# Cross-attention and a mixture of experts on one core: the last group's four pairs of sends, each begun half a tile after the one before

## The chip, the core and the metric

The kernel runs on one core of a Trainium2 chip. The metric is the time of one execution on the device in microseconds; lower is better. The core's engines are called PE (matrix multiply; PEld is its loading of weights), DVE (vector), ACT (scalar), POOL (GpSimd) and SP (which here only issues DMAs). Each runs its own list of instructions in order, and they wait for each other through semaphores.

## The reference

Eight sequences of 256 rows of 256 numbers pass through a gated cross-attention and then a gated mixture of experts. Everything is float32.

```python
# _L0_ffn_ref: x is (8, 256, 256), W1 (8, 1024, 256), W2 (8, 256, 1024), Wr (8, 256)
logits = jnp.einsum('btd,ed->bte', x, Wr)
probs = jax.nn.softmax(logits / TEMPERATURE, axis=-1)
topk_vals, topk_idx = jax.lax.top_k(probs, TOPK)            # TOPK = 2 of 8 experts
router_weights = topk_vals / topk_vals.sum(-1, keepdims=True)
one_hot = jax.nn.one_hot(topk_idx, E, dtype=x.dtype)
gate = jnp.einsum('btk,btke->bte', router_weights, one_hot)
h = jax.nn.silu(jnp.einsum('btd,efd->btef', x, W1))
y = jnp.einsum('btef,edf->bted', h, W2)
out = jnp.einsum('bte,bted->btd', gate, y)

# the whole
x = x + jnp.tanh(g_xattn[0]) * _L0_xattn_ref(_layernorm(x), ctx_1024, ...)
x = x + jnp.tanh(g_ffn[0]) * _L0_ffn_ref(_layernorm(x), W1, W2, Wr)
```

The attention (16 heads, 120 context rows) comes first and is not touched by the change. In the second half the reference runs all experts for all 2048 tokens and weighs them; only two of eight weights of a token are not zero.

## The kernel before

**Routing.** The kernel computes an expert only for the tokens that chose it. Tokens are handled in four groups of 512 (`g` from 0 to 3; the last is `g = NG - 1 = 3`). For a group, `logits` and `router` choose two experts for each token. `places` (L302 to L380) then works out the row that each token gets in the list of each of its two experts, and sends the token's normalised row (256 numbers, its gates and its number) to that row of the table `routed` in DRAM. A list has 2048 rows for each expert.

A send is an indirect DMA on POOL (L366) that scatters 128 rows. There are eight for a group: two halves `h` of the group, for each the first and the second choice, for each two blocks of 128 tokens. `places` is a generator. Each step of it makes one reduction on DVE (L362, row numbers of two blocks, tile `slot0` or `slot1`), issues the two sends that use it, and yields. So a group is four steps of one reduction and two sends; below, the four pairs are S1, S2, S3 and S4. The code ahead of the first reduction (counts by two matmuls, gates, row numbers) runs in the first step.

**Tiles of the second half.** The loop at L1213 goes over `order`, tiles of 128 rows of one expert. The first eight are the first 128 rows of each expert's list (`"first"`); the lists are laid out so that these rows are filled by the groups 0 and 1, and their loads are declared independent of later sends. From `i = 8` on come `"full"` tiles, whose place in the lists and whose expert are known only when all groups are counted: `table()` (L710) works them out on DVE in four steps, the first up to L737, the second from L670 to L744 with the tiles `full_row` and `expert_i`, and two more for the rest of the rows. Their loads (`load`, L845 and L852 on SP) read `full_row` into a register and must come after all sends.

One pass `i` of the loop, in the order of the code:

- L1241 `go_up()`: up projection of tile `i`, 16 matmuls (L897), and its Silu on ACT (L905)
- L1255 `open_tile(i + 1)`: the rows of the next tile are transposed on DVE (L884); for a full tile its expert's weights are copied first (L864)
- L1259: for `i` 5 and 8, a step of the table
- L1274 `close_tile()`: down projection of tile `i - 1`, 8 matmuls (L913), scaling by the gate on DVE (L921), and the sum into the output by an indirect DMA on POOL (L938, `add_up`)
- L1284: for `i` 3 and 4, two steps of the last group's sends
- L1287: for `i` 4, the first step of the table
- L1296: loads of tiles up to four ahead, on SP

The order of the instructions of PE, DVE, ACT and SP is that of the code. POOL has no order of its own written out; it too ends up with its instructions in the order in which the code makes them. So before the change POOL has, from pass 3 on: sum of tile 2, S1, S2, sum of tile 3, S3, S4, sum of tile 4, sum of tile 5. Each sum waits for the landing of the sum before it. DVE has the reductions of S1 and S2 directly one behind the other after the gates (pass 3), and those of S3 and S4 behind the scaling of tile 3 and ahead of the table's first step (pass 4).

Of the kernel before, what the change touches and what calls it, by code (L numbers as in the profile page):

```python
# [49 lines left out]
def tile_gated_xattn_moe(  # L50
# [356 lines left out]
    def load_expert(e):  # L407
        nc.sync.dma_start(
            part(e, 0, DC, DFF), w1T[e].rearrange("(c p) f -> p c f", p=P)
        )  # L410
        nc.sync.dma_start(
            part(e, DC * DFF, FC, D), w2T[e].rearrange("(c p) d -> p c d", p=P)
        )
# [231 lines left out]
    def turn_y(b, bank):  # L645
        g, i = b // 2, b % 2
        rows, xn2T = groups[g]
        turned(xn2T[:, :, ts(i, N)], [rows[i][:, k, :D] for k in range(2)], f"f{b}", bank)
# [161 lines left out]
    def load(t):  # L810
        kind, i = t
        xt = take(fp, [P, XW], "xt", f"xt_{kind}{i}", bufs=6)
        if kind == "first":
            for first in load_blocks(xt, i * T):
                for send in behind:
                    tc.declare_no_dep(
                        first.ins, send.ins, reason="rows behind those of the first tiles"
                    )
                firsts.append(first)
            return xt  # L820
        if kind == "quad":
            nc.gpsimd.indirect_dma_start(
                out=xt,
                out_offset=None,
                in_=routed[:, :],
                in_offset=bass.IndirectOffsetOnAxis(
                    ap=tables[1][0][:, i : i + 1], axis=0
                ),
            )
            return xt  # L830
        start = nc.sync.value_load(
            tables[0][1][0:1, i : i + 1], min_val=0, max_val=NOWHERE
        )
        load_blocks(xt, start)
        return xt
# [19 lines left out]
    def weights(t, xt):  # L855

        kind, i = t
        if kind != "full":
            w2 = part(i, DC * DFF, FC, D)
            return part(i, 0, DC, DFF), xt[:, D + i : D + i + 1], lambda: w2  # L860
        expert_i = tables[0][0]
        e = nc.vector.value_load(expert_i[0:1, i : i + 1], min_val=0, max_val=E - 1)
        w1 = take(fw[0], [P, DC, DFF], "w1", f"w1_{i}")
        nc.vector.tensor_copy(  # L864
            w1.rearrange("p c f -> p (c f)"),
            w_sb[:, ds(e, 1), : DC * DFF].rearrange("p e f -> p (e f)"),
        )
        gate = take(fw[3], [P, 1], "gate", f"gate_{i}", bufs=4)
        nc.vector.tensor_copy(gate, xt[:, D : D + E][:, ds(e, 1)])

        def copy_w2():
            w2 = take(fw[0], [P, FC, D], "w2", f"w2_{i}")
            nc.vector.tensor_copy(
                w2.rearrange("p c d -> p (c d)"),
                w_sb[:, ds(e, 1), DC * DFF :].rearrange("p e f -> p (e f)"),
            )
            return w2

        return w1, gate, copy_w2

    def turn(t, xt):
        if t[0] != "quad":
            xT = take(fp, [P, DC, P], "xT", f"xT_{t[0]}{t[1]}")
            nc.vector.transpose(xT.rearrange("p c n -> p (c n)"), xt[:, :D])  # L884
            return xT
        tr = take(ps_tr, [P, DC, P], "tr", f"xtT_{t[0]}{t[1]}")
        for c in range(DC):
            nc.tensor.transpose(tr[:, c, :], xt[:, ts(c, P)], ident)
        xT = take(fp, [P, DC, P], "xT", f"xT_{t[0]}{t[1]}")
        nc.vector.tensor_copy(xT, tr)  # L890
        return xT

    def up(t, xT, w1):
        ph = take(fw[1], [P, FC, P], "ph", f"ph_{t[0]}{t[1]}")
        for f in range(FC):
            for c in range(DC):
                nc.tensor.matmul(  # L897
                    ph[:, f, :],
                    lhsT=w1[:, c, ts(f, P)],
                    rhs=xT[:, c, :],  # L900
                    start=(c == 0),
                    stop=(c == DC - 1),
                )
        hT = take(fw[3], [P, FC, P], "hT", f"hT_{t[0]}{t[1]}")
        nc.scalar.activation(hT, ph, AF.Silu)  # L905
        return hT
# [3 lines left out]
    def down(t, hT, gate, xt, w2):  # L910
        py = take(fw[2], [P, 512], "mm", f"py_{t[0]}{t[1]}")
        for f in range(FC):
            nc.tensor.matmul(  # L913
                py[:, :D],
                lhsT=hT[:, f, :],
                rhs=w2[:, f, :],
                start=(f == 0),
                stop=(f == FC - 1),
            )
        y = take(fw[3], [P, D], "y", f"y_{t[0]}{t[1]}")  # L920
        nc.vector.tensor_scalar(y, py[:, :D], gate, None, ALU.mult)  # L921
        add_up(t, y, xt)
# [125 lines left out]
    def open_tile(t, xt):  # L1048
        state["ready"] = t, xt, weights(t, xt), turn(t, xt)
# [6 lines left out]
    def go_up():  # L1056

        t, xt, (w1, gate, _), xT = state["ready"]
        return t, up(t, xT, w1), gate, xt
# [8 lines left out]
    picked, sending = {}, {}  # L1068
# [32 lines left out]
    for s, (b, o, nb) in enumerate(units):  # L1101
        k = 2 * o + nb
        n = b + 1
        g = b // 2 - 1
# [107 lines left out]
    g = NG - 1  # L1212
    for i, t in enumerate(order):  # L1213
        if i == 12:

            with tc.If(more > 0):  # L1216
                spare = {}
                for j in range(SPARE):
                    tj = ("full", j)
                    xt = load(tj)  # L1220
                    w1, gate, copy_w2 = weights(tj, xt)
                    w2 = copy_w2()
                    down(tj, up(tj, turn(tj, xt), w1), gate, xt, w2)
                for j in range(MIXED, QUADS):
                    for _ in quad(j, load(("quad", j))):
                        pass
                spare = None
        if i == 10:
            more = nc.values_load(tables[1][3][0:1, 0:1], min_val=0, max_val=FULLS)
        w2_of = state["ready"][2][2]  # L1230
        if i == 2:
            turn_y(B - 1, bank_tr)

        mixed = mix <= i < mix + 4 * MIXED
        if i == mix - 1:
            quads = [quad(j, xt) for j, xt in enumerate(quad_xts)]
        if mixed and i % 4 == 0:
            running = quads[(i - mix) // 4]
        if mixed and i > mix:
            next(running)  # L1240
        new = go_up()  # L1241
        if i == mix - 1:
            next(quads[0])
        copies = []
        if i == 1:
            for k in range(2):
                copies.append(wide_out(B - 1, k, ps_py))
        if i == 2:
            lg = logits(g, groups[g][1], bank_tr)
            next(lg)  # L1250
        for k, copy in enumerate(copies):
            copy()
            norm_y(B - 1, k)
        if i + 1 < len(order):
            open_tile(order[i + 1], xts[i + 1])  # L1255
        if mixed:
            next(running)

        if i in (5, 8):  # L1259
            tables.append(next(parts))  # L1260
        if i == 6:
            next(parts)
        if i == 0:
            norms_y.finish()
            weigh(B - 1, 1, ps_py)
            load_expert(4)
            turn_y(B - 2, bank_tr)
            sending[g - 1] = places(g - 1, groups[g - 1][0], picked[g - 1], bank_tr)
        if i == 3:
            sending[g] = places(g, groups[g][0], picked[g], bank_tr)  # L1270
        w2 = w2_of()
        if i == 1:
            norms_y.finish()
        close_tile()  # L1274
        state["pending"] = *new, w2
        if mixed:
            next(running)
        if i == 2:
            lg = next(lg)
            picked[g] = router(g, lg)  # L1280
        if i < 2:
            for _ in range(2):
                next(sending[g - 1])
        if 2 < i < 5:  # L1284
            for _ in range(2):
                next(sending[g])
        if i == 4:  # L1287
            parts = table()
            next(parts)
            routing_pool.close()  # L1290
            qp.append(
                ctx.enter_context(
                    tc.tile_pool(name="quads", bufs=1, side="right", reuse_waits="tile")
                )
            )
        while len(xts) <= min(i + AHEAD, len(order) - 1 if tables else 7):  # L1296
            xts[len(xts)] = load(order[len(xts)])
        if i == mix - 4:
            quad_xts = [load(("quad", j)) for j in range(MIXED)]
        if i == 1:  # L1300
            load_expert(3)
            load_expert(7)
# [44 lines left out]
```

## Time and profile before

| | |
|---|---|
| median of 3 runs | 538.94 us (537.75 to 539.55) |
| the profiled execution | 538.01 us |
| its span on the core | 536.30 us |
| mean granted PE clock in it | 0.992 |
| instructions | 10503 |
| sends (L366) | 32, 995 ns mean on POOL |
| sums of first and full tiles (L938) | 31, 1552 ns at the least |

A row of a timeline gives the start and the duration of a group of instructions in microseconds from the start of the span, the engine, the source line, the operation, what it writes and reads, the count, and in brackets the idle time of the engine ahead of it with what ended it. "issue" means that the profile shows nothing that the engine waited for. "SPq" is SP issuing a DMA; the transfer itself goes on after that. A POOL row of a send or a sum is the time in which POOL makes the transfer's descriptors, not the transfer.

The granted clock is the share of its full clock that PE was allowed. Of the page, two rows give it over the whole span, in 40 slices of 13.4 us:

```
PE   8999999999999999999999998999999999999992
PEclk9999999999999999999999998999999999999998
```

### The profile page before, as it was taken

To read this page: it belongs to the slowest core of one execution; us is meant where nothing else is said; L and a number is where in the kernel's file an instruction comes from. 1 tells how busy PE (TensorE), PEld (TensorE's weight loads), DVE (VectorE), ACT (ScalarE), POOL (GpSimd) and SP (SyncE) were. 2 spreads that over 40 slices of the span, in tenths; PEclk is the share of its full clock that TensorE was granted. 3 is DMA by queue.
4 is the path that set the end of the run, shared out by engine and by line. 5 is a ranking of instruction groups with operands and counts; after the bars stand their busy time and mean duration, and the time that the engine had idled before them with its cause. 6 is when DMAs were issued, how large, how long until landed. Compare 5 with 4: busy or idle time off the path is not lost. (4 is left out here: it accounts for less than half of the span.)

```text
span 536.3 us, 10503 instructions
## 1 busy us (share of the span) xinstructions
PE 520.9 (97%) x3636; PEld 438.5 (82%) x3636; DVE 283.9 (53%) x683; ACT 220.1 (41%) x700; POOL 127.8 (24%) x135
## 2 busy tenths in 40 slices
PE   8999999999999999999999998999999999999992
PEld 7788887878878788787889996999997787889991
DVE  3675656567765567744673446444544454443530
ACT  1666546464554654557630310111144554601110
POOL 2011100000332003310013445222331224234332
PEclk9999999999999999999999998999999999999998
DMA  8999990140420501012059784333322221422321
GB/s 294 333 308 309 299 261 24 46 151 2 165 93 31 188 2 40 32 41 41 2 174 376 224 240 85 44 44 45 45 41 31 32 33 16 49 36 26 44 27 20
DMA packets 82156, 57.57 MB, mean 107 GB/s; under 512 B 42864, under 2 KB 77168, under 8 KB 82096
## 3 DMA queue, kind: packets, MB, share of 16 engines
q1 hardware_dynamic: 75200, 47.36, 31.9%
q0 software_dynamic: 6480, 8.81, 9.3%
q10 hardware_dynamic: 416, 0.66, 0.4%
q8 instruction: 30, 0.49, 0.4%
q14 instruction: 30, 0.25, 0.1%
HBM read 28.67 MB, written 28.27 MB: 106 GB/s over the span
## 5 line engine op out<-in xcount | busy, mean ns | idle before, releaser
L575 ACT ACTIVATE pr<-psc,mx 128x120 f32<-128x120 f32 x256 | 88.8, 373 | 65.3 <-DVE mx L569 63.3
L897 PEld LDWEIGHTS ph_full<-xT_full,w 128*128 128x128 f32 x736 | 85.1, 192 | 6.4 <-issue 5.0
L897 PE MATMUL ph_full<-xT_full,w 128*128 128x128 f32 x736 | 86.8, 276 | 0.3 <-PEq L1216 0.3
L913 PE MATMUL py_full<-w,hT_full 128*128 128x256 f32 x368 | 83.1, 379 | 0.0
L913 PEld LDWEIGHTS py_full<-w,hT_full 128*128 128x128 f32 x368 | 68.2, 190 | 8.4
L525 PE MATMUL pq<-xnT,w_sb 128*128 128x256 f32 x256 | 62.7, 388 | 0.4 <-DVE xnT L208 0.4
L938 POOL DMA_INDIRECT out_dram<-y_full,xt_full x23 | 38.9, 1691 | 99.2 <-DVE y_full L921 65.3
L905 ACT ACTIVATE hT_full<-ph_full 128x1024 f32<-128x1024 f32 x23 | 23.5, 1023 | 94.1 <-PE ph_full L897 94.1
L619 PE MATMUL pw<-w_sb 128*128 128x256 f32 x256 | 58.5, 382 | 0.0
L575 ACT ACTIVATION_READ_ACCUMULATOR pr<-psc,mx 128x1 f32 x256 | 55.8, 218 | 0.0
L525 PEld LDWEIGHTS pq<-xnT,w_sb 128*128 128x128 f32 x256 | 46.6, 190 | 10.8 <-issue 3.1
L619 PEld LDWEIGHTS pw<-w_sb 128*128 128x128 f32 x256 | 47.7, 190 | 9.0 <-issue 2.5
L563 DVE TENSOR_REDUCE mx<-psc 128x8 f32<-128x960 f32 x32 | 37.0, 1155 | 31.3 <-PE psc L555 31.3
L366 POOL DMA_INDIRECT routed<-rows,slot x32 | 31.8, 995 | 55.7 <-DVE slot L362 49.0
L921 DVE TENSOR_SCALAR y_full<-py_full,gate 128x256 f32<-128x256 f32 x23 | 11.1, 483 | 61.6 <-PE py_full L913 55.7
L595 ACT COPY w_sb<-tr 120x512 f32<-120x512 f32 x64 | 34.7, 598 | 19.8 <-PE tr L594 19.8
L584 DVE TENSOR_TENSOR pr<-pr,sm 128x960 f32<-128x960 f32 x32 | 37.0, 1158 | 1.1
L555 PE MATMUL psc<-kT,w_sb 64*128 64x120 f32 x512 | 37.2, 284 | 0.0
L985 ACT COPY part<-w_sb 128x1024 f32 x32 | 31.1, 1045 | 13.5 <-PE py_q L1024 13.0
L555 PEld LDWEIGHTS psc<-kT,w_sb 64*128 64x128 f32 x512 | 31.1, 187 | 6.4 <-issue 3.6
L864 DVE COPY w<-w_sb 128x2048 f32 x23 | 28.5, 1240 | 12.0 <-issue 4.9
L594 PEld LDWEIGHTS tr<-ident,pr 128*120 128x120 f32 x256 | 29.5, 138 | 5.7 <-issue 3.3
(173 smaller groups left out, 652.1 us busy)
## 6 DMA issues: line engine op xcount, KB each, us to landing
routed<-w_sb SPq DMA_DIRECT2D x8, 2120.0 KB
w_sb<-in_w1T_dram SPq DMA_DIRECT2D x8, 1024.0 KB
w_sb<-in_w2T_dram SPq DMA_DIRECT2D x8, 1024.0 KB
xt_full<-routed SPq DMA_DIRECT2D x184, 16.0 KB
out_dram<-x SPq DMA_DIRECT2D x8, 256.0 KB
x<-in_x_dram SPq DMA_DIRECT2D x7, 256.0 KB
w_sb<-in_w_kv_dram SPq DMA_DIRECT2D x3, 512.0 KB
w_sb<-in_w_q_dram SPq DMA_DIRECT2D x2, 512.0 KB
```

The source lines that it names most:

```text
L366: send = nc.gpsimd.indirect_dma_start(out=routed[:, :], out_offset=bass.IndirectOffsetOnAxis(ap=slot[:, i : i + 1], axis=0), in_=rows[h][: ...
L525: nc.tensor.matmul(pq[:, i, :], lhsT=wq_sb[:, c, ts(2 * h + i, P)], rhs=xnT[:, c, :], start=(c == 0), stop=(c == DC - 1),)
L555: nc.tensor.matmul(psc[:, j, ts(i, M)], lhsT=qT[ts(j, DH), 4 * o + i, ts(nb, P)], rhs=kT[ts(j, DH), 4 * o + i, :], start=True, stop=True,)
L563: nc.vector.tensor_reduce(mx.rearrange("p (j i) -> p j i", i=4), psc[:, :, : 4 * M].rearrange("p j (i m) -> p j i m", m=M), AX.X, ALU.max,)
L575: nc.scalar.activation(pr[:, h, :], psc[:, j, ts(i, M)], AF.Exp, bias=mx[:, h : h + 1], scale=QK_SCALE, accum_out=sm[:, h : h + 1],)
L584: nc.vector.tensor_tensor(pr, pr, sm.unsqueeze(2).to_broadcast([P, 8, M]), ALU.mult)
L595: nc.scalar.copy(pT_sb[:, ts(j, 4), ts(nb, P)], tr[:M, :, :])
L619: nc.tensor.matmul(pw[:, :D], lhsT=oT_sb[b % 2][:, ci, ts(k, P)], rhs=wo_sb[:, ci, :], start=(ci == 0), stop=(ci == IC - 1),)
L897: nc.tensor.matmul(ph[:, f, :], lhsT=w1[:, c, ts(f, P)], rhs=xT[:, c, :], start=(c == 0), stop=(c == DC - 1),)
L913: nc.tensor.matmul(py[:, :D], lhsT=hT[:, f, :], rhs=w2[:, f, :], start=(f == 0), stop=(f == FC - 1),)
L938: add = nc.gpsimd.indirect_dma_start(out=out[:, :], out_offset=bass.IndirectOffsetOnAxis(ap=slots[:, k : k + 1], axis=0), in_=y[own, :], i ...
L985: nc.scalar.copy(w[:, q, :].rearrange("p (a b) -> p a b", b=D if down else DFF // 2), slab[:, ts(h, FC // 2), :] if down else slab[:, :, t ...
```

## The change

The four steps of the last group are spread. Before, two steps are taken at the end of pass 3 and two at the end of pass 4. After, one is taken at the end of pass 3, one in pass 4 between the transpose of tile 5 and the down projection of tile 3, one at the end of pass 4, and one in pass 5 between the transpose of tile 6 and the table's second step.

```diff
@@ for i, t in enumerate(order):
         if mixed:
             next(running)
 
+        if i in (4, 5):
+            next(sending[g])
+
         if i in (5, 8):
             tables.append(next(parts))
         if i == 6:
@@
         if i < 2:
             for _ in range(2):
                 next(sending[g - 1])
-        if 2 < i < 5:
-            for _ in range(2):
-                next(sending[g])
+        if i in (3, 4):
+            next(sending[g])
         if i == 4:
             parts = table()
             next(parts)
```

`next(sending[g])` runs `places` to its next yield: one reduction (L362) on DVE and two sends (L366) on POOL.

## The prediction

> **What bounds the kernel now.** I read four views in this order: the busy times, the timeline of PE around the sends of the last group, the granted clock there, and then POOL, DVE and SP for the instructions that the change touches. Tiles of the last loop are counted from 0, as `i` is.
>
> The first line says that there is one engine to watch:
>
> ```profile
> PE 520.9 (97%) x3636; PEld 438.5 (82%) x3636; DVE 283.9 (53%) x683; ACT 220.1 (41%) x700; POOL 127.8 (24%) x135
> ```
>
> An edit elsewhere is worth something only where it makes PE start a matmul at another time. In the timeline of PE there is one place after the start of the kernel where it loses microseconds, and it lies right where the change is:
>
> ```profile
> 322.45 3.73 PE L897 MATMUL ph_first<-xT_first,w_sb 128*128 128x128 f32 x32
> 326.07 0.59 PE L913 MATMUL py_first<-w_sb,hT_first 128*128 128x256 f32 x2
> ...
> 334.13 3.73 PE L897 MATMUL ph_first<-xT_first,w_sb 128*128 128x128 f32 x32
> 337.70 3.62 PE L913 MATMUL py_first<-w_sb,hT_first 128*128 128x256 f32 x16
> 341.16 3.73 PE L897 MATMUL ph_full<-xT_full,w 128*128 128x128 f32 x32
> ```
>
> Columns are start, duration, and the group. Start to start, an up projection (L897) takes 337.70 - 334.13 = 3.57 us and a down projection (L913) 341.16 - 337.70 = 3.46 us, so a tile is 7.03 us. The down projection of tile 5, begun at 326.07, takes 334.13 - 326.07 = 8.06 us: 4.60 us are lost. Nothing that it needs is late; the idle time inside it is put down to "issue". Its neighbour ACT shows that PE's results are seen late too:
>
> ```profile
> 331.42 1.02 ACT L905 ACTIVATE hT_first<-ph_first 128x1024 f32<-128x1024 f32 x1 [10.03 <-remote]
> 337.96 1.03 ACT L905 ACTIVATE hT_first<-ph_first 128x1024 f32<-128x1024 f32 x1 [5.51 <-PE ph_first L897]
> ```
>
> In a quiet tile the Silu starts 337.96 - 334.13 = 3.83 us after the up projection; in tile 6 it starts 331.42 - 322.45 = 8.97 us after it, 5.14 us late; in tile 5 (315.34 to 320.37, in the same two timelines) 5.03 us after it, 1.20 us late. The clock follows (window, length, busy time of PE, PEld, DVE, ACT, POOL, then granted clock, DMA share, GB/s):
>
> ```profile
> 329.00:330.00 1.00, 0.31 (x1) 0.32 (x2) 0.90 (x4) 0.00 (x0) 1.00 (x1) 0.87 0.42 136
> 330.00:333.00 3.00, 2.79 (x7) 1.73 (x7) 0.60 (x4) 1.02 (x1) 0.57 (x1) 0.50 0.51 60
> 333.00:334.00 1.00, 1.00 (x6) 0.90 (x5) 0.00 (x0) 0.00 (x0) 0.00 (x0) 0.93 0.24 31
> ```
>
> That is 0.13 + 3 x 0.50 + 0.07 = 1.70 us of clock withheld, a part of the 4.60 at most. All of it falls into the stretch in which POOL issues the eight sends and two sums without a pause:
>
> ```profile
> 314.98 1.56 POOL L938 DMA_INDIRECT out_dram<-y_first,xt_first  x1 [8.59 <-issue]
> ...
> 319.42 0.96 POOL L366 DMA_INDIRECT routed<-rows,slot  x1 [0.30 <-issue]
> ...
> 326.40 0.96 POOL L366 DMA_INDIRECT routed<-rows,slot  x1 [0.30 <-issue]
> ```
>
> Call the four pairs S1 to S4. POOL's order is: sum of tile 2 (314.98), S1 (316.84), S2 (319.42), sum of tile 3 (321.95), S3 (323.86), S4 (326.40 and 327.67), sum of tile 4 (328.93). POOL stood for 8.59 us ahead of the sum of tile 2 and is behind with everything from there on.
>
> **The change part by part.** In the built programs PE, ACT, POOL and SP run the same instructions in the same order with the same waits; so do all DMAs. On DVE the reductions that make the row numbers of S2 and of S4 move back, and nothing else. The reader should see in DVE's timeline where they stood:
>
> ```profile
> 309.71 0.27 DVE L362 TENSOR_REDUCE slot<-oh 128x2 int32<-128x16 f32 x2
> 310.18 0.45 DVE L884 STREAM_TRANSPOSE xT_first<-xt_first 128x256 f32<-128x256 f32 x1 [0.21 <-issue]
> ...
> 315.80 0.23 DVE L362 TENSOR_REDUCE slot<-oh 128x2 int32<-128x16 f32 x2
> ...
> 320.23 0.45 DVE L884 STREAM_TRANSPOSE xT_first<-xt_first 128x256 f32<-128x256 f32 x1 [2.21 <-DMA xt_first<-routed]
> ```
>
> *S2's reduction* goes behind the transpose of tile 5. It ended at 309.71 + 0.27 = 309.98; now it ends some 0.45 us and two small gaps later, near 310.7. POOL reaches S2 at 319.42, so 8.7 us of POOL's backlog hide it, and the two sends start when they did. The transpose itself comes about 0.1 us earlier, for PE at 315.34: nothing.
>
> *S4's reduction* goes behind L715 to L737 of the table and behind the transpose of tile 6, which waits for that tile's rows until 320.23. It ended at 316.03; now it ends at 320.23 + 0.45 + 0.16 (one reduction, by its row's median of 160 ns), near 320.9. POOL reaches S4 at 326.40: 5.5 us of cover. Without this cover each us more would delay S4, the sum behind it, and then SP, which stands here until S4 has landed:
>
> ```profile
> 330.38 4.09 SPq L845 DMA_DIRECT2D xt_full<-routed  x8
> ```
>
> Those are the rows of tile 8, transposed by 337.05 and wanted by PE at 341.16, another 4.11 us of cover.
>
> *What is behind the moved reductions on DVE.* L715 to L737 come 0.1 us earlier and run into the same wait for rows, so they give nothing. The rest of the table (320.64 to 325.57) comes about 0.16 us later. Who waits: SP for `full_row` (written at 325.25, but SP stands until 330.38 for the landing); POOL for y of tile 4 (begun at 325.49, wanted at 328.93, 3.0 us to spare); PE for the transpose of tile 7 (325.89, wanted at 334.13, or at 329.53 if the stall were gone: 3.2 us to spare). With all cover gone it would be 0.16 us, 0.03%.
>
> *What I cannot price from a row is the stall.* It is known only as it stands. From below it can go entirely: -4.60, of which tile 8 gives back 0.49 (its transpose ends at 337.05, PE would want it at 341.16 - 4.60 = 336.56), so -4.1. From above: lateness grew by 5.14 - 1.20 = 3.94 us over the two phases from up of tile 5 to up of tile 6, 2.0 a phase, so one phase more is +2.0. Between these I take 0, because the nearest row is POOL's own run of sends, which keeps order and start times.
>
> A rule speaks against the change here. The sends above took 0.96 us at 319.42, where DVE was idle (from 318.02 to 320.23), and 0.96 at 326.40, where it ran without a pause: DVE's work did not lengthen them. The Trainium skill ("DMA: Bandwidth & Descriptors", section "SWDGE vs HWDGE vs iDMA") says that GpSimd writes descriptor rings in SBUF and that DVE locks it out of SBUF in its two-port mode. If that held for these reductions, the one that now falls among the sends would hold POOL by its own 0.16 us, and the time would be 539.1 instead of 538.9.
>
> The half clock came although no gap between PE's groups in this stretch is over 1.22 us. The Trainium skill ("TensorE: Matmul & The Clock Gate", section "Why this matters for your kernels") sets the limit for idle gaps near 3 us; by it the 1.70 would not be here to win or lose, by the trace they are.
>
> **Sum.** The profiled execution has a span of 536.30 and took 538.01, 1.71 around it. 538.01 + 0 (S2) + 0 (S4) + 0 (table) = 538.01; the median of the runs shown is 0.93 higher, so the forecast on their scale is 538.9.
>
> **The rivals.**
> *The pauses take the stall away (faster).* That is the case in which the change does spread the sends, which my forecast denies: POOL has to wait for a reduction, and PE catches up in the pause. For it: four sends in a row ahead of 298.27 cost PE nothing (its down projection from 297.03 is followed by the next up projection at 300.70, 3.67 us later), and eight with two sums among them do. Against it: the pause needs the reduction of S4 later than 326.40, 5.5 us later than I place it. Price: -4.1 for all, 534.8; -1.7 if only the clock stays up, 537.2.
>
> *S4's signal comes late and the run of sends gets longer (slower).* Before, the reduction of S4 signalled at 316.03, ahead of the first send; now it signals in the middle of the sends, where PE's signals to ACT came 1.20 and 5.14 us late. If DVE's signal to POOL is as late as the worst of these, it is there at 320.9 + 5.1 = 326.0, only 0.4 ahead of POOL. The point from which it decides is 5.5 us of lateness: from there S4 and the sum behind it slip, PE's stall goes on for up to another phase, and the time is 538.9 + 2.0 = 540.9. Against it: DVE's own chain of L670 to L744, each step waiting for the one before, ran through the sends at 0.7 us and less a step.
>
> **How the numbers follow.** No change that can be seen: 0.64; its own range is 537.3 to 540.5, as 0.3% (1.6 us) is about what a measurement of this kernel can tell from no change. Faster by more: 0.15. Slower by more: 0.21, above the faster one since the moved instructions can only come later at POOL and there are few places where PE could gain. The range 536.8 to 541.2 holds the likeliest case, the clock-only part of the faster one and the slower one at its full price; the stall gone (some 0.1) and a stall longer by more than a phase (some 0.08) are left out.
>
> **What would show it.** Right: in the changed kernel S1 to S4 start with 1.27 us between sends as before, S4 over 4 us behind its reduction; the reductions of L362 stand alone behind two of the transposes; a down projection near the end of the sends still takes about 8 us. Wrong: POOL idle before S2 or S4 with a DVE slot as releaser; SP's first load of `xt_full` earlier or later than about 330 by more than 1 us; the long down projection back at 3.5 us, or a second long one behind it.

## The result and the profile after

| | before, run beside it | after |
|---|---|---|
| median (lowest to highest), 22 runs each | 538.67 us (535.15 to 542.62) | 538.14 us (536.29 to 542.05) |
| ratio after to before, 95% interval | | 0.9999 (0.998 to 1.0017) |
| the profiled execution, and its span | 538.01 us, 536.3 us | 538.78 us, 537.1 us |

The change makes no difference that can be measured: the interval reaches 0.2% to either side of 1. The medians differ by 0.1%, the means (538.58 before, 538.50 after) by 0.02%. The span of the profiled execution is 0.8 us longer, but that is not the change: the sum of tile 0 on POOL, ahead of everything that was moved, already starts 0.73 us later (300.79 against 300.06), S1 0.79 us later (317.63 against 316.84), and tile 8's up projection, behind all that was moved, 0.72 us later (341.88 against 341.16). So both traces are compared from S1 on, by distances and not by absolute times.

POOL's timeline of the kernel after:

```profile
315.77 1.56 POOL L938 DMA_INDIRECT out_dram<-y_first,xt_first  x1 [8.61 <-issue]
317.63 0.99 POOL L366 DMA_INDIRECT routed<-rows,slot  x1 [0.30 <-DVE scratch L728]
...
320.22 0.96 POOL L366 DMA_INDIRECT routed<-rows,slot  x1 [0.30 <-issue]
...
327.19 0.96 POOL L366 DMA_INDIRECT routed<-rows,slot  x1 [0.30 <-issue]
```

S1 starts at 317.63, S2 at 320.22, S4 at 327.19: 2.59 and 9.56 us after S1. Before it was 319.42 - 316.84 = 2.58 and 326.40 - 316.84 = 9.56. The four pairs of sends are not spread at all. The 0.30 us ahead of each send also stands where nothing was waited for, so a name behind it is only the last signal that came in.

DVE's timeline of the kernel after shows what did move:

```profile
310.19 0.17 DVE L362 TENSOR_REDUCE slot<-oh 128x2 int32<-128x16 f32 x1
310.57 0.45 DVE L884 STREAM_TRANSPOSE xT_first<-xt_first 128x256 f32<-128x256 f32 x1 [0.20 <-DMA w_sb<-in_w2T_dram]
310.94 0.13 DVE L362 TENSOR_REDUCE slot<-oh 128x2 int32<-128x16 f32 x1
...
316.29 0.16 DVE L362 TENSOR_REDUCE slot<-oh 128x2 int32<-128x16 f32 x1
...
320.89 0.45 DVE L884 STREAM_TRANSPOSE xT_first<-xt_first 128x256 f32<-128x256 f32 x1 [2.29 <-DMA xt_first<-routed]
321.26 0.13 DVE L362 TENSOR_REDUCE slot<-oh 128x2 int32<-128x16 f32 x1
```

The reductions of S2 and S4 stand alone behind the transposes. S2's ends at 311.07 and POOL wants it at 320.22: 9.15 us of cover. S4's ends at 321.39 and POOL wants it at 327.19: 5.80 us.

PE's timeline, then ACT's, of the kernel after:

```profile
322.94 3.73 PE L897 MATMUL ph_first<-xT_first,w_sb 128*128 128x128 f32 x32
326.51 1.51 PE L913 MATMUL py_first<-w_sb,hT_first 128*128 128x256 f32 x6
329.04 0.59 PE L913 MATMUL py_first<-w_sb,hT_first 128*128 128x256 f32 x2 [1.02 <-issue]
...
334.15 4.44 PE L897 MATMUL ph_first<-xT_first,w_sb 128*128 128x128 f32 x32
338.42 3.62 PE L913 MATMUL py_first<-w_sb,hT_first 128*128 128x256 f32 x16
```

```profile
332.21 1.02 ACT L905 ACTIVATE hT_first<-ph_first 128x1024 f32<-128x1024 f32 x1 [11.45 <-remote]
```

The stall is there as before, in the same phase. The down projection of tile 5 takes 334.15 - 326.51 = 7.64 us, 4.18 more than a quiet one, and the up projection behind it 338.42 - 334.15 = 4.27 instead of 3.57: 4.88 us lost in all, against 4.60 before. The Silu of tile 6 starts 332.21 - 322.94 = 9.27 us after the up projection began, 5.44 us later than in a quiet tile (5.14 before). The Silu of tile 5 is not late this time: it starts at 319.74, 3.91 us after its up projection (315.83), where before it was 5.03.

The windows of the kernel after (columns as in the prediction) and SP's timeline:

```profile
330.00:333.00 3.00, 1.70 (x6) 1.27 (x6) 1.33 (x6) 0.79 (x1) 1.37 (x1) 0.87 0.55 85
333.00:334.00 1.00, 1.00 (x4) 0.82 (x3) 0.00 (x0) 0.23 (x1) 0.00 (x0) 0.50 0.46 64
334.00:341.00 7.00, 7.00 (x45) 6.62 (x45) 2.31 (x4) 1.02 (x1) 1.65 (x1) 0.89 0.36 45
```

```profile
331.16 4.09 SPq L845 DMA_DIRECT2D xt_full<-routed  x8
```

The clock withheld is 3 x 0.13 + 0.50 + 7 x 0.11 = 1.66 us, against 1.70 before; it comes some 2 us later, which is why it now lies in the up projection. SP's loads of tile 8 begin 13.53 us after S1 (331.16 - 317.63), before 13.54 (330.38 - 316.84).

### The profile page after: what moved, and what is told of

It is laid out like the page before. It is cut to its first block, busy times and chain, and to the rows that moved or that the text cites. A ratio compares the mean times of both kernels' runs of the same rounds, so it can differ in the third digit from the quotient of the medians.

```text
span 537.1 us, 10503 instructions
## 1 busy us (share of the span) xinstructions
PE 521.3 (97%) x3636; PEld 439.8 (82%) x3636; DVE 284.7 (53%) x683; ACT 219.3 (41%) x700; POOL 127.4 (24%) x135
## 5 line engine op out<-in xcount | busy, mean ns | idle before, releaser
L913 PE MATMUL py_full<-w,hT_full 128*128 128x256 f32 x368 | 83.1, 379 | 0.0
L913 PEld LDWEIGHTS py_full<-w,hT_full 128*128 128x128 f32 x368 | 68.2, 190 | 8.4
L366 POOL DMA_INDIRECT routed<-rows,slot x32 | 31.8, 995 | 55.6 <-DVE slot L362 48.9
```

Source lines behind the costliest of these rows:

```text
L366: send = nc.gpsimd.indirect_dma_start(out=routed[:, :], out_offset=bass.IndirectOffsetOnAxis(ap=slot[:, i : i + 1], axis=0), in_=rows[h][: ...
L913: nc.tensor.matmul(py[:, :D], lhsT=hT[:, f, :], rhs=w2[:, f, :], start=(f == 0), stop=(f == FC - 1),)
```

## The experiments

Two theories were to be told apart. The first is the forecast's: POOL's backlog hides the later reductions, and the stall belongs to POOL's run of sends, which the change leaves as it is. The second: the reductions' place does matter (a late signal to POOL, or a stall that depends on how the sends lie), and two effects cancel in the result.

There were three series. The first ran on one chip, the other two on another. In all three series the kernel before took less time than beside the result, where its median was 538.67: medians 534.72 (23 runs), 534.75 (23) and 535.0 (17). Every ratio is against the runs of the same series.

### No sends, or half of them, in the last group (first series)

Both are edits of the kernel before.

```diff
                 for i in range(2 * h, 2 * h + 2):
+                    if g == NG - 1:
+                        continue
                     send = nc.gpsimd.indirect_dma_start(
```

> The eight sends of the last group (S1 to S4) are left out, the reductions stay; the rows of that group's tokens never reach the lists, so their expert part is missing from the output. Theory (the unbroken run of sends and sums on POOL makes PE's stall): no down projection of a first tile takes over 4 us start to start, the Silu of tile 6 starts about 3.8 us after its up projection instead of 9, and the span is 4 us or more shorter than the 536 to 537 of the kernel before. Rival (the stall belongs to what DVE does there, the chain of the table, or to PE's own code loading): the down projection of tile 5 still takes about 8 us and the span stays within 1.5 us, since all of that is still there.

The second kernel leaves out S3 and S4 alone (`if g == NG - 1 and h == 1`).

> Only S1 and S2 of the last group are sent; S3 and S4 are left out, so half of that group's tokens lack their expert part. Theory: four sends and two sums make a run half as long; PE's signals are late by 2 to 3 us at most, as after the four sends of the group before (2.6 us), and no phase is lengthened by more than 0.5 us; the span is 4 us shorter. If lateness is by time from the first send, the up projection of tile 5 is still seen 1.2 us late and that of tile 6 not at all. Rival (the stall hangs on the place, not on the run): about 8 us for the down projection of tile 5 as before.

Measured, one execution each: 532.65 us without the sends, 533.38 with half of them. PE's timeline of the kernel without any of the last group's sends (its line numbers are 2 higher):

```profile
326.11 3.62 PE L915 MATMUL py_first<-w_sb,hT_first 128*128 128x256 f32 x16
329.56 3.73 PE L899 MATMUL ph_first<-xT_first,w_sb 128*128 128x128 f32 x32
333.13 3.62 PE L915 MATMUL py_first<-w_sb,hT_first 128*128 128x256 f32 x16
336.59 3.73 PE L899 MATMUL ph_full<-xT_full,w 128*128 128x128 f32 x32
```

No stall, and no wait at tile 8. With half of the sends it is the same (326.37, 329.83, 333.40, 336.85). Taken alone this would look like proof that the sends make the stall. It is none, because the kernels with all sends show no stall in this series either.

### The sum of tile 2 held back behind S1 and S2 (first series)

This does spread the sends. On the kernel before, `add_up` of tile 2 is issued behind the two steps of pass 3 and forced behind them in POOL's order, so that S1 and S2 no longer wait in POOL's queue for that sum.

```diff
-        add_up(t, y, xt)
+        if t == order[2]:
+            held.append((t, y, xt))
+        else:
+            add_up(t, y, xt)
...
+        if i == 3:
+            add_up(*held.pop())
...
```

> Nothing left out: the sum of tile 2, which holds up POOL for 8.6 us, is put behind S1 and S2 on POOL. Theory: S1 starts near 310, 6 to 7 us earlier; S1 and S2 run while POOL would stand; the sum of tile 2 at 315 and of tile 3 at about 318 make pauses, S4 ends near 325 instead of 329. If an unbroken run is what stalls PE, the stall is below 1 us and the time 4 us shorter (ratio 0.992). If it is the number of sends in some 15 us whatever the pauses, half of the stall stays (ratio 0.996). Rival (the place): ratio 1.000.

Measured: 534.37 us (533.41 to 535.63, 12 runs), ratio 0.9989 (0.9972 to 1.0006). S1 starts at 310.29, S3 only at 322.65, with 3.77 us of POOL idle between. SP's loads of tile 8 start at 329.52, and PE starts tile 8 without a wait (333.19 to 336.64 is one quiet down projection). The gain is not clear of 1; the stall that it was to break up was not there to break.

### S4's reduction later, behind the table's second step (first series)

On the kernel after, S4's step goes behind L670 to L744 in pass 5.

```diff
-        if i in (4, 5):
+        if i == 4:
             next(sending[g])
 
         if i in (5, 8):
             tables.append(next(parts))
+        if i == 5:
+            next(sending[g])
```

> The changed kernel with S4's reduction moved on by another 5 us of DVE's work, behind the table's second step, where it ends at 325.8 to 326.5 on the scale of the kernel before. Same order on POOL. Theory (POOL's backlog covers up to 5.5 us): POOL reaches S4 at 326.4 to 327.2, so S4 starts at its old time or at most 0.5 us later, and the time is that of the kernel before (ratio 0.998 to 1.002). Rival (signals raised among the sends come up to 5 us late): POOL waits up to 5 us at S4, SP's first load of a full tile goes from 330.4 to 333 or later, and the time is 1 to 3 us longer.

Measured: 534.61 us (534.05 to 536.31, 10 runs), ratio 1.0000 (0.9982 to 1.0018). DVE's, POOL's and PE's timelines of this kernel:

```profile
325.25 0.16 DVE L362 TENSOR_REDUCE slot<-oh 128x2 int32<-128x16 f32 x1
```

```profile
326.66 0.96 POOL L366 DMA_INDIRECT routed<-rows,slot  x1 [0.30 <-DVE scratch L750]
```

```profile
326.79 3.62 PE L913 MATMUL py_first<-w_sb,hT_first 128*128 128x256 f32 x16
330.25 3.73 PE L897 MATMUL ph_first<-xT_first,w_sb 128*128 128x128 f32 x32
```

The reduction ends at 325.41, 8.31 us after S1's start, where in the kernel after it was 321.39 - 317.63 = 3.76; S4 still starts 326.66 - 317.10 = 9.56 us after it. Even with 1.25 us of cover POOL does not wait. In this execution DVE's signal thus came less than 1.25 us late, beside the 5.5 us from which the slower rival would have decided. The sends and sums run unbroken from 317.10 to 330.8, and PE still has no stall.

### Both kernels again, and the kernel without sends again (second series)

No edit; the question was whether the stall is there at all.

> The kernel before once more, to see whether PE's stall belongs to the kernel or to the chip it was on. The four runs so far on a second chip had no stall, the one with all eight sends in an unbroken row included. If the stall is the chip's or the moment's: here the down projection of tile 5 takes 3.5 us or 8 us as the chip has it, and the time is 534.7 or 538.7 with it. If it is the program's (something that all four edited kernels moved): about 8 us and 538 to 539 again.

> The changed kernel beside it on the same chip. Theory: same as the kernel before on this chip, ratio 0.998 to 1.002, with the stall in both or in neither. Rival (the moved reductions decide whether there is a stall): one of the two has the 8 us down projection and the other not, and the times differ by about 4 us.

> The last group's sends left out again, on this chip. If before_again shows a stall here: theory (the sends cause it where the chip allows it) no stall, 4 us and more shorter; rival, the stall stays. If before_again shows none, the time is 2 us below it or less, from what else the sends cost.

Measured: before 534.17 us in one execution; after 534.79 (533.72 to 537.58, 11 runs), ratio 1.0008 (0.9995 to 1.0021); without the sends 533.23. PE's and POOL's timelines of the kernel before in this series:

```profile
326.02 3.62 PE L913 MATMUL py_first<-w_sb,hT_first 128*128 128x256 f32 x16
329.48 3.73 PE L897 MATMUL ph_first<-xT_first,w_sb 128*128 128x128 f32 x32
333.05 3.62 PE L913 MATMUL py_first<-w_sb,hT_first 128*128 128x256 f32 x16
337.24 3.81 PE L897 MATMUL ph_full<-xT_full,w 128*128 128x128 f32 x32 [0.58 <-DVE xT_full L884]
```

```profile
326.58 0.96 POOL L366 DMA_INDIRECT routed<-rows,slot  x1 [0.30 <-DVE scratch L748]
```

The down projection at 326.02 takes 3.46 us, the same phase that took 8.06 us in the execution of the prediction. POOL's row is S4, 326.58 - 317.01 = 9.57 us after S1: the same run of sends. PE now reaches tile 8 earlier, at 333.05 + 3.46 = 336.51, and waits for its rows until 337.24: 0.73 us. The span is 532.5, so 536.3 - 532.5 = 3.8 us less, and 4.60 - 0.73 = 3.87. The stall and what tile 8 gives back are the whole difference between the two executions. The kernel after has no stall here either (its down projection of tile 5 runs from 326.11 to 329.57), and POOL does not wait at S4.

In the same trace of the kernel after, S4's reduction falls into a send. DVE's and POOL's timelines:

```profile
320.65 0.13 DVE L362 TENSOR_REDUCE slot<-oh 128x2 int32<-128x16 f32 x1
```

```profile
320.55 0.96 POOL L366 DMA_INDIRECT routed<-rows,slot  x1 [0.30 <-issue]
```

The send, from 320.55 to 321.51, holds the reduction whole and takes 0.96 us, like the sends around it.

### S4 itself later: behind the sum of tile 4 (second series)

On the kernel after, S4's step moves to the end of pass 5, so that POOL has the sum of tile 4 ahead of it. This is the only kernel in which POOL starts S4 later.

```diff
-        if i in (4, 5):
+        if i == 4:
             next(sending[g])
...
-        if i in (3, 4):
+        if i in (3, 4, 5):
             next(sending[g])
```

> The changed kernel with the whole step of S4 (reduction and sends) at the end of pass 5: on POOL S4 comes behind the sum of tile 4, so it really starts later, by one sum, about 1.9 us. Theory: SP's first load of a full tile starts 1.9 us later (332.2 instead of 330.4). With the stall in PE the 4.1 us of cover hide it, ratio 1.000; without the stall tile 8 has no cover and PE waits 1.4 to 2.0 us ahead of its up projection, ratio 1.003 to 1.004. Rival (full tiles have slack that the profile does not show): ratio 1.000 without a stall too.

Measured: 536.88 us (535.73 to 541.85, 12 runs), ratio 1.0054 (1.0034 to 1.0074). POOL's, SP's and PE's timelines of this kernel:

```profile
326.30 1.60 POOL L938 DMA_INDIRECT out_dram<-y_first,xt_first  x1 [0.48 <-DVE scratch L750]
328.20 1.15 POOL L366 DMA_INDIRECT routed<-rows,slot  x1 [0.30 <-DVE scratch L685]
329.66 0.96 POOL L366 DMA_INDIRECT routed<-rows,slot  x1 [0.30 <-issue]
```

```profile
332.33 3.95 SPq L845 DMA_DIRECT2D xt_full<-routed  x8
```

```profile
333.00 3.62 PE L913 MATMUL py_first<-w_sb,hT_first 128*128 128x256 f32 x16
339.08 3.81 PE L897 MATMUL ph_full<-xT_full,w 128*128 128x128 f32 x32 [2.46 <-DVE xT_full L884]
```

S4 starts 328.20 - 316.55 = 11.65 us after S1 instead of 9.57, SP's loads come at 332.33 instead of 330.59, and PE, due at tile 8 at 336.46, starts at 339.08. It waits 2.62 us, 1.89 more than in the kernel before of this series; the spans differ by 534.4 - 532.5 = 1.9. The expectation had a wait of 1.4 to 2.0 us; it is longer by the 0.73 us that the kernel before already waits without a stall. The chain S4, landing, SP's loads, tile 8 is real. A later start of S4 drives it, and the kernel after does not move that start. S4's first send takes 1.15 us here instead of 0.96; why is not shown.

### All sends of the last group first (third series)

On the kernel before, all four steps are taken at the end of pass 3, and the sum of tile 2 is forced behind S4.

```diff
-        if 2 < i < 5:
-            for _ in range(2):
+        if i == 3:
+            for _ in range(4):
                 next(sending[g])
+        if i == 3:
+            add_up(*held.pop())
...
```

> Nothing left out: all four steps of the last group at the end of pass 3, and the sum of tile 2 on POOL behind S4, so that the eight sends run from 310 to 320 while POOL would stand for the sum's turn. Theory (without the stall, S4's landing is what tile 8 waits for): SP's first load of a full tile starts when full_row is there and read, near 326 instead of 330.6, PE's wait at tile 8 goes, and the time is 0.4 to 0.8 us shorter (ratio 0.9985 to 0.9993). With the stall on this chip and the sends as its cause: it moves to 312 to 322 and keeps its size, ratio 1.000. Rival (the sums put off cost as much, the sum of tile 2 holding the buffers of tile 8's rows and of a later y): PE waits at another tile, ratio 1.000 or above.

> The kernel before a third time, as the measure for the two beside it. With the stall: time near 538, a down projection of 8 us. Without: near 534.5, no such phase, and PE waits 0.3 to 0.8 us for the transpose of tile 8, whose rows come late since SP stands until S4 has landed.

> The last group's sends left out once more, beside before_third. With a stall in before_third: theory (the sends cause it) none here and 4 us or more shorter; rival (they don't) the stall stays. Without one: 1 to 2 us shorter than before_third, 0.7 of it the wait at tile 8.

Measured: 534.31 us (533.17 to 535.76, 12 runs), ratio 0.9990 (0.9978 to 1.0002); before, one execution, 534.67; without the sends 532.91. POOL's and PE's timelines of the kernel with all sends first (L913 is L914 in it):

```profile
310.68 0.99 POOL L366 DMA_INDIRECT routed<-rows,slot  x1 [2.99 <-DVE slot L362]
...
319.58 0.96 POOL L366 DMA_INDIRECT routed<-rows,slot  x1 [0.30 <-issue]
```

```profile
333.57 3.62 PE L914 MATMUL py_first<-w_sb,hT_first 128*128 128x256 f32 x16
337.03 3.73 PE L897 MATMUL ph_full<-xT_full,w 128*128 128x128 f32 x32
```

The last send begins at 319.58, SP's loads at 327.82 instead of 330.49, and the wait at tile 8, 1.13 us in the kernel before of this series, is gone: 337.03 - 333.57 = 3.46. The gain of 0.7 us in the medians is less than that wait, and the interval just takes in 1, so it is not shown. Neither this kernel nor the one with tile 2's sum held back is shown to be faster than the kernel before.

## Why the prediction was right

**"POOL's backlog hides S2's and S4's reductions": right, and tested.** Forecast 8.7 and 5.5 us of cover, measured 9.15 and 5.80. The reduction 4.5 us later still costs nothing that can be measured, while a later S4 costs 0.54% (both without a stall). That the change doesn't spread the sends it is named after is what both traces show.

**"S4's signal comes late and the run gets longer" (the slower rival): did not happen.** POOL has its 0.30 us ahead of S4 in every trace in which S4 kept its place. With the stall present the lateness is bounded by the kernel after, at 5.80 us or less; without it by the later reduction, at less than 1.25.

**"The rest of the table 0.16 us later, hidden": hidden is right, the 0.16 us is not resolved.** From tile 6's transpose to L744 it is 326.18 - 320.89 = 5.29 us after and 325.38 - 320.23 = 5.15 before, 0.14 more. In the second series it is 5.17 after against 5.24 before, 0.07 less. Nothing of it reaches PE.

**"A rule speaks against the change": not seen.** A send with the reduction wholly inside it took 0.96 us, the same as without it, so the 0.16 us were not added. The one send of the last group that took longer than 1.00 us, 1.15 in the kernel with S4 behind the sum, has no reduction of L362 in it. The Trainium skill ("DMA: Bandwidth & Descriptors", section "SWDGE vs HWDGE vs iDMA") has DVE lock GpSimd out in its two-port mode; for this reduction no run here shows such a lock.

**"The stall, from -4.1 to +2.0, taken as 0": right for the result, in part by luck.** It was 4.60 before and 4.88 after, in the same phase, with 1.70 and 1.66 us of clock withheld. That the stall stood in both profiles is not owed to POOL's order alone, as the next point shows. The size from below was about right: -4.60 with 0.49 given back at tile 8 makes -4.1 in the forecast, and between two executions of the same kernel it was -3.8 with 0.73 given back. The size from above, 2.0 us for each phase, was read from lateness that grew from 1.20 to 5.14; in the kernel after it goes from 0.08 to 5.44, so there is no such steady growth. The gap of 1.22 us that the prediction names is one of PE's weight loads; the longest between matmuls there is 0.95.

**What failed is the reason given for the stall.** The prediction tied it to "the stretch in which POOL issues the eight sends and two sums without a pause", and its faster rival said that pauses would take it away. The unbroken run alone does not make it: the same eight sends and two sums, at the same distances, ran without a stall in the profiles of the kernel before (second and third series), of the kernel after (second series) and of the one with the later reduction (first series). A hint that something else was different in the earlier executions stands ahead of the last group's sends: DVE's copy of `plT`, which PE begins at 296.46 in both. Here it is in the kernel before as predicted from, and then in the second series:

```profile
299.13 0.29 DVE L228 COPY lgT<-plT 128x128 f32<-128x128 f32 x1 [5.34 <-remote]
```

```profile
297.17 0.29 DVE L228 COPY lgT<-plT 128x128 f32<-128x128 f32 x1 [3.38 <-PE plT L220]
```

In the first, DVE starts 2.0 us later, behind the four sends of the group before (293.40 to 298.27). From PE's start to DVE's it is 2.67 us there and 2.70 in the kernel after, the two profiles with a stall, and 0.71 in all eleven without one; in those two the profile names "remote" and no engine as what ended DVE's wait. So in the two executions with a stall an engine was already late at PE's result before the last group was sent. What in the chip, its surroundings or the moment does this stays open. PE's code loading, the rival named with the first experiment, is not seen to differ: the two instruction queues (q8 and q14) move one packet each near the phase, at 324 to 326 and at 327 to 328, in the kernel before with the stall and, in the second series, without it. Whether the sends are needed for the stall, and whether pauses between them would remove it, could not be seen with a stall present: none of the eleven profiles of the experiments has one. What "pauses take the stall away" was worth is therefore neither shown nor refuted; what is shown is that this change makes no pauses.

## What to carry to other kernels

An edit that moves the producer of an operand moves nothing while the consumer's engine is behind with its queue; compare the producer's end with the time at which that engine gets there, and to move the consumer, change what stands ahead of it on its own engine. A stall that the profile puts down to "issue" may belong to the executions and not to the program: profile the unchanged kernel a second time, elsewhere, before an explanation is built on it. Without a stall, all sends of the last group together are worth 1.5 to 2.1 us (534.72 to 532.65, 534.75 to 533.23, 535.0 to 532.91, each a median against one execution), so by estimate no placing of them brings more than 0.4%.

## What was not expected of the hardware

One program on one core took 538.67 us in the median beside the result and 534.72 to 535.0 in three later series, 0.7% less, with a 4.60 us stall of PE in its profile beside the result and none in its profiles of the second and third series. In the kernel after, ACT started up to 5.44 us late behind PE during the stall.

PE's clock fell to half although in this stretch PE was never idle for more than 0.95 us at a time in the prediction's trace and 1.02 in that of the kernel after. There PE was busy for 1.30 of the 4 us from 328 to 332, the granted clock still 1.00, and behind them the clock was 0.60 in one us and 0.50 in the next. In the kernel before of the second series, where these gaps are missing, the granted clock is 1.00 from 326 to 341. The Trainium skill ("TensorE: Matmul & The Clock Gate", section "Why this matters for your kernels") warns of idle gaps over about 3 us; here several short ones within a few us went with the same loss.
